# A fused block with paged attention on one core: two chunks of transposed heads per store, and the output weights on another DMA queue

## The chip, the cores and the metric

The kernel runs on one core of a Trainium2 chip. The metric is device time in microseconds of one execution, as the median of several runs. Beside it one execution was recorded by the hardware profiler; its span runs from its first to its last instruction. The engines are called by the profile's names: PE (matmul), PEld (its weight loads), DVE, ACT, POOL, and SP, which only issues DMAs here. A row "SPq" or "ACTq" is a DMA issue on that engine's instruction stream.

## The reference

There are 32 sequences of 32 tokens with 512 features. Four layers are each added to their input:

```python
x = x + einsum('bct,bcd->bdt', x, W0[cond])                    # token mixing, one of 16 matrices
x = x + x @ W.T + 0.5 * (x @ A[label]) @ Bw.T                  # base weights and a low-rank part
x = x + einsum('bsi,boi->bso', x, W2[adapter])                 # one of 8 adapters per sequence
# attention: 32 query heads, 8 key heads of 128, 512 cached keys in 16 pages of 32, 32 new ones
q, k, v = x @ Wq.T, x @ Wk.T, x @ Wv.T
q, k = rope(rmsnorm(q) * wq, pos), rope(rmsnorm(k) * wk, pos)
scores = q @ concat(k_cache[block_table], k).T / sqrt(128)     # cached keys beyond the length masked
x = x + (softmax(scores) @ concat(v_cache[block_table], v)) @ Wo.T
```

All of it is in float32.

## The kernel before, in words

The 1024 token rows are held as `NT` = 8 tiles of 128 rows, so that one tile holds `BT` = 4 sequences. The program has two stages, called A and attention below.

**Stage A** first computes the first three layers and then the projections. The projected width is cut into 12 chunks of 512 columns (`NCH`): chunks 0 to 7 are queries, 8 and 9 are keys, 10 and 11 are values. One chunk holds four heads (`REP`). Query and key chunks are computed in pairs of chunks by pairs of tiles. One such block takes seven products (`M_ORDER`) instead of eight, the results of which are added up on ACT, DVE and POOL. `BLOCKS` lists 20 blocks: the first pair of chunks is that of the keys (8, 9), the other four are queries. Time is counted in slots, one per product, seven per block. `at(slot, ...)` files a piece of work under a slot, and `flush(slot)` issues what is filed there. The queues of PE, DVE, ACT, POOL and SP follow that order as written.

A block yields four units: two chunks (`c0`, `c1`) for two tiles. `formed`, `by_cos`, `by_sin` and `rotated` make the rotated heads `u.a` of a unit (128 tokens by four heads of 128). `store_heads` (line 484) then transposes them on DVE in squares of 32 (line 489) into a tile `st`, of which there are four, and stores them with four DMAs, one per sequence, from SP (line 498). They go to a scratch array in DRAM, `q_d` for queries and `k_d` for keys, which is laid out with the head dimension first, as attention needs it. For a block that begins at slot g, the four query units are stored at g+6, g+9, g+11 and g+13; key units at g+9, g+11, g+14 and g+15. Every fourth chunk, `store_inverses` also writes the norms of the queries to `r_d` (line 459). Among the same slots SP loads the key pages of sequences 0 and 1 (`load_page`, line 199). ACT issues the stores of projected values (`v_d`, line 326) and the loads of weight pairs (`w_pair`).

**Attention** is one loop over `n`, a step per sequence `b` and key head `g`: 256 steps, and eight more (`LAG`) in which the last ones drain. A step issues, in this order: the transfers of a coming sequence; the scores of (b, g) on PE (lines 998, 999); the masked copy of them on DVE (line 1007) and the exponential on ACT (line 1023); `fill`, a matmul pair of the projection of the last value chunk, left over for steps up to 36 (line 318), whose result ACT copies and stores; the loads of output weights; `place`, which transposes a quarter of the probabilities of four steps ago on DVE (line 1036) and copies it on ACT, POOL and DVE into `placed` (lines 1048, 1050, 1052); `share`, a piece of the output projection (line 1153), from step 37 (`BEGIN`); and the products of the probabilities with the values of eight steps ago (line 1076).

What SP issues in the steps of sequence b: at its first step the second half of its queries `qt` (line 229), four pieces of new values `vn` (line 268), the new keys of b+1 (line 224) and 12 of the 16 key pages of b+1 (line 199), for which it reads page numbers from a table; at its fifth step the first half of the queries of b+1, four pieces of the norms `rq` (line 236), the remaining four pages and the next table. POOL issues the gathers of cached values `vt` (line 256). Keys and values have two sets of buffers, one for even and one for odd sequences.

**The output weights** are held in two tiles: `wos[0]` with the rows of the first 20 of 32 positions, `wos[1]` with the last 12. Each is loaded in 16 parts (`load_wo`, line 895), one per (r, k), where r picks a group of 32 partitions and k one of four rows in turn. A part of the first tile is 320 KB, of the second 192 KB. The memory of `wos[0]` was part of stage A's (among it the tiles `st`), so its first load has to wait until that is free. `WO_AT` (line 1208) says in which steps parts of the first tile are loaded: two in each of steps 4 to 8, one in steps 10, 14, 18, 22, 26 and 30, all of them issued from ACT. The second tile is loaded from SP, one part per step, from step 37 on.

Of the kernel before, what the change touches and what calls it, by code (L numbers as in the profile page):

```python
# [20 lines left out]
P = 128  # L21
# [17 lines left out]
QUAD = 4  # L39
# [20 lines left out]
def cond_resid_kernel(  # L60
# [420 lines left out]
                u.a[:, h, :], u.a[:, h, :], AF.Copy, scale=u.ss[:, h : h + 1]  # L481
            )

    def store_heads(u):
        c, t, a = u.c, u.t, u.a


        st = tp.tile([P, D // S, REP, S], F32, tag="st", name=f"st_{c}_{t}", bufs=4)
        nc.vector.transpose(
            st.rearrange("p k h s -> p h k s"), a.rearrange("p h (k d) -> p h k d", d=S)  # L490
        )
        if c < HQ // REP:
            dst, c0 = q_d, c * REP * S
        else:
            dst, c0 = k_d, (c - HQ // REP) * REP * S
        for j in range(BT):
            r = slice(j * S, (j + 1) * S)
            nc.sync.dma_start(
                out=dst[t * BT + j, :, c0 : c0 + REP * S].rearrange("(k d) x -> d k x", d=S),
                in_=st[r].rearrange("p k h s -> p k (h s)"),  # L500
            )

# [9 lines left out]
    def block(n: int, i: int, p: int):  # L512
        c0, c1 = PAIRS[i]
        u11, u12 = unit(n, c0, 2 * p), unit(n, c1, 2 * p)
        u21, u22 = unit(n, c0, 2 * p + 1), unit(n, c1, 2 * p + 1)
        q = u11.q
        b = SimpleNamespace()
        g = 7 * n

        def begin(m):  # L520
            if m in (2, 4):
                pool = ps_n
            else:
                pool = ps_m
            return pool.tile([P, HID], F32, tag="mm", name=f"m{m}_{i}_{p}")

        def out_of(name, ps, tag, bufs):
            t = rp.tile([P, HID], F32, tag=tag, name=f"{name}_{i}_{p}", bufs=bufs)
            nc.scalar.copy(t, ps)  # L529
            setattr(b, name, t)  # L530

        def mm(m):
            if m == 1:
                b.X = begin(1)
                product(b.X, i, p, 1)
            elif m == 5:
                b.Z = begin(5)
                product(b.Z, i, p, 5)
            elif m in (2, 4):
                ps = begin(m)  # L540
                setattr(b, "Y" if m == 2 else "W", ps)
                product(ps, i, p, m)
            else:
                product(b.Z if m == 3 else b.X, i, p, m, True)

        V, G = nc.vector, nc.gpsimd

        at(g + 1, lambda: out_of("r1", b.X, "r", 2))
        at(g + 2, lambda: out_of("r5", b.Z, "r5", 1))
        at(g + 3, lambda: formed(u11, b.r1, b.Y, V))  # L550
        at(g + 3, by_cos, u11)
        at(g + 4, lambda: out_of("r2", b.X, "r", 2))
        at(g + 4, by_sin, u11, 0)
        at(g + 4, by_sin, u11, 1)
        at(g + 5, lambda: formed(u12, b.r2, b.Z, V))
        at(g + 5, by_cos, u12)
        at(g + 5, rotated, u11)
        at(g + 6, lambda: out_of("r3", b.X, "r", 2))
        at(g + 6, by_sin, u12, 0)
        at(g + 6, by_sin, u12, 1)  # L560
        at(g + 7, lambda: formed(u21, b.r3, b.W, V))
        at(g + 7, by_cos, u21)
        at(g + 7, lambda: formed(u22, b.r3, b.r5, G))
        at(g + 8, rotated, u12)
        at(g + 8, by_sin, u21, 0)
        at(g + 8, by_cos, u22)
        at(g + 9, by_sin, u21, 1)
        at(g + 9, by_sin, u22, 0)
        at(g + 10, by_sin, u22, 1)
        at(g + 10, rotated, u21)  # L570
        at(g + 11, rotated, u22)
        if q:
            for u, o, hs in (
                (u11, 5, (0, 1, 2)),
                (u11, 6, (3,)),
                (u12, 7, (0, 1, 2)),
                (u12, 8, (3,)),
                (u21, 8, (0,)),
                (u21, 9, (1, 2)),
                (u21, 10, (3,)),  # L580
                (u22, 10, (0, 1)),
                (u22, 11, (2, 3)),
            ):
                at(g + o, squares, u, hs)
            at(g + 6, store_heads, u11)
            at(g + 9, store_heads, u12)
            at(g + 11, store_heads, u21)
            at(g + 13, store_heads, u22)
            half, odd = divmod(c1, QUAD)
            if odd == QUAD - 1:  # L590
                for t in (2 * p, 2 * p + 1):
                    at(g + 12, query_roots, half, t)
                    at(g + 13, query_inverses, half, t)
                    at(g + 13, store_inverses, half, t)
        else:
            for u, o in ((u11, 5), (u12, 7), (u22, 10), (u21, 11)):
                at(g + o, squares, u)
                at(g + o + 1, key_sums, u)
                at(g + o + 2, key_roots, u)
                at(g + o + 2, key_inverses, u)  # L600
                at(g + o + 3, key_scales, u, G if u is u22 else nc.scalar)
                at(g + o + 4, store_heads, u)
        if n + 1 < len(BLOCKS):
            at(g + 6, load_factors, n + 1, 0 if BLOCKS[n + 1][0] else 1, BLOCKS[n + 1][1])
        return mm
# [283 lines left out]
    def wo(h: int):  # L889
        return wos[0][:, h, :] if h < HQ - LATE else wos[1][:, h - (HQ - LATE), :]  # L890

    def load_wo(i: int, r: int, k: int, eng=nc.sync):
        g0 = i * (HQ - LATE) // REP
        w = wos[i][r * S : (r + 1) * S].rearrange("d (g k) o -> d g k o", k=REP)[:, :, k, :]
        eng.dma_start(out=w, in_=w_o4[r, k][:, g0 : g0 + w.shape[1], :])

    vnp = ctx.enter_context(tc.tile_pool(name="b_vn", bufs=2, side="right"))
    qp = ctx.enter_context(tc.tile_pool(name="b_q", bufs=2, side="right"))
# [306 lines left out]
    EMPTY = tuple(n for n in range(LAG + 2, FILLED) if n % 2 == 0)  # L1205
    EMPTY = EMPTY[: FILLED - len(fills)]
    filled = {}
    WO_AT = dict.fromkeys(range(QUAD, LAG + 1), 2) | dict.fromkeys(range(10, 31, 4), 1)
    wo_parts = [divmod(i, REP) for i in range(REP * REP)]

    def fill(n: int):
# [15 lines left out]
    with tc.manual_schedule(engines=order):  # L1227
        for n in range(N + LAG):
            b, g = divmod(n, HK)
            if n == FILLED:  # L1230
                pa.close()
                late = ctx.enter_context(tc.tile_pool(name="b_w", bufs=1))
                places.append(late)
                wos[1] = late.tile([P, LATE, HID], F32, name="wo_1")
            if BEGIN <= n <= N and n % (BT * HK) == 0:

                load_residual((n - BEGIN) // (BT * HK))
            if n < N:
                if g == 0 and b >= 1:
                    load_queries(b, 1)  # L1240
                    load_new_values(b)
                if g == 0 and 1 <= b < B - 1:
                    load_keys(b + 1)
                    keys = Picked(nc.sync, k_cache, pages_of.pop(b + 1), page_keys(b + 1), K_SHAPE)
                    load_new_keys(b + 1)
                    keys.transfer(slice(0, 12))
                if g < L // P and b >= 2:
                    load_value_chunk(b, g)
                if g == QUAD and b < B - 1:
                    load_queries(b + 1, 0)  # L1250
                    load_inverses(b + 1)
                    if b >= 1:
                        keys.transfer(slice(12, NPP))
                    if 1 <= b < B - 2:
                        load_table(b + 2)
                scored = scores(b, g)
                exponentials(*scored)
            flip_kept(n)
            fill(n)
            if n == QUAD + 1:  # L1260
                load_new_values(0)
            if n in WO_AT:
                for _ in range(WO_AT[n]):
                    load_wo(0, *wo_parts.pop(0), nc.scalar)
            if 0 <= n - FILLED < REP * REP:
                load_wo(1, *divmod(n - FILLED, REP))
            if QUAD <= n < N + QUAD:
                bq, i = divmod(n - QUAD, HK)
                q, j = divmod(i, QUAD)
                if j == 0:  # L1270
                    gather_new(bq, q)
                if j == 2:
                    flip_new(bq, q)
                place(bq, q, j)
            share(n)
            if n >= LAG:
                values(*units[n - LAG])
            if n < N and g == HK - 1 and b < B - 1:
                see_keys(b + 1)
            if n > N + QUAD:  # L1280
                at = 4 * (n - N - QUAD - 1)
                finish(NT - 1, range(at, at + 4))
        assert not dens and not prs and not pos and not placed and not pns
        load_residual(NT - 1)
        flip_kept(N + LAG)
        finish(NT - 1, range(3 * QUAD, HALF))
        finish_by_halves(NT - 1)
# [76 lines left out]
```

## Time and profile before

| | |
|---|---|
| Median of 3 runs | 1187.63 us (1181.24 to 1188.65) |
| Profiled execution, its time | 1189.01 us |
| Its span | 1187.2 us |
| PE, DVE, ACT, POOL busy | 96%, 68%, 63%, 47% of the span |
| Mean granted PE clock | 0.978 |
| Attention's first scores | 374.87 us |
| Bytes read and written in DRAM | 220.07 MB, 29.49 MB |

An engine's busy share is an average over stages with different limits, and PE's counts matmuls whose ends are modelled. The chain that ended last is PE for 50% of the span, and the rest of it is hardly split. So the page's line of 40 slices and busy times by stretch say more than the shares.

In the answers quoted below, a line of a timeline is: start in us, duration in us, engine, line, operation, tiles (written <- read), count of instructions merged, and in brackets the idle time before it and what ended it. A line of waits is: who waited, for whom, us in total, times, longest. The releaser is inferred: where the engine or transfer named has nothing to do with the instruction, something stands before it in the same queue.

### The profile page before, as it was taken

How to read it: one execution, taken by the hardware profiler on the slowest of the kernel's cores; microseconds unless marked ns; L12 is line 12 of the kernel's file. 1: busy time of each engine (PE TensorE's matmuls, PEld its weight loads, DVE VectorE, ACT ScalarE, POOL GpSimd, SP SyncE). 2: the span in 40 equal slices, each digit the busy share in tenths (PEclk: the TensorE clock that was granted, in tenths of full speed). 3: DMA queues.
4: the chain of work that ended last, by engine and by line, in shares of the span. 5: the costliest groups of instructions: out<-in, count | busy, mean ns of one | idle time of the engine just before them, and what ended most of it. 6: DMA issues, size and time to landing. Idle time of an engine off the chain costs nothing.

```text
span 1187.2 us, 19830 instructions
## 1 busy us (share of the span) xinstructions
PE 1137.2 (96%) x5432; PEld 737.7 (62%) x5432; DVE 807.1 (68%) x1670; ACT 751.6 (63%) x1900; POOL 554.3 (47%) x709
## 2 busy tenths in 40 slices
PE   8999999999999388899899999999999999999998
PEld 5543444444444176677677777777777777777766
DVE  2510788898775256677577778778877877877860
ACT  1211477666666176677577877777777777877760
POOL 3400788998985343334343443344344344333410
PEclk9999999999999698899899999999999999999999
DMA  8997456755465667689767667766776776776710
GB/s 325 389 407 305 171 138 209 220 118 161 103 178 141 165 165 228 202 264 247 213 210 238 218 220 230 242 218 211 260 218 197 257 224 197 241 238 206 225 46 10
DMA packets 193426, 250.93 MB, mean 211 GB/s; under 512 B 33794, under 2 KB 153218, under 8 KB 187554
## 3 DMA queue, kind: packets, MB, share of 16 engines
q1 hardware_dynamic: 166818, 160.64, 44.0%
q0 software_dynamic: 19216, 69.35, 17.5%
q10 hardware_dynamic: 7280, 19.66, 5.1%
q8 instruction: 44, 0.72, 0.2%
q14 instruction: 68, 0.56, 0.2%
HBM read 220.07 MB, written 29.49 MB: 210 GB/s over the span
## 4 chain that ended last, share of the span: by engine, by line
PE 50%; SPq 3%; DVE 2%; issue 1%; DMA 1%; POOL 0%; ACT 0%; ACTq 0%; DVEq 0%
PE f_ps L1153 16%; PE o_ps L1076 15%; PE s_ps L998 9%; PE s_ps L999 7%; PE o_ps L1096 1%; SPq L199 1%; DMA kt<-in_k_cache_dram 1%; SPq L187 1%; DVE turned L1036 1%; SPq L236 1%; PE f_ps L1173 1%; PE f_ps_last L1173 1%; DVE ot L1133 0%; PE pn_ps L1063 0%; DVE pr L1007 0%
## 5 line engine op out<-in xcount | busy, mean ns | idle before, releaser
L1048 ACT COPY placed<-turned 32x512 f32<-32x512 f32 x539 | 332.1, 616 | 55.8 <-DVE turned L1036 23.0
L1076 PEld LDWEIGHTS o_ps<-vt,placed 128*128 128x128 f32 x2048 | 270.8, 194 | 125.7 <-issue 98.1
L1007 DVE CUSTOM_DVE_ANT_0 pr<-s_ps,mask,rq 128x544 f32<-128x544 f32 x256 | 200.6, 784 | 153.9 <-PE s_ps L999 145.7
L1076 PE MATMUL o_ps<-vt,placed 128*128 128x128 f32 x2048 | 274.4, 278 | 10.2 <-ACT placed L1048 3.2
L1050 POOL COPY placed<-turned 32x512 f32<-32x512 f32 x268 | 163.5, 610 | 256.2 <-DVE turned L1036 197.4
L1023 ACT ACTIVATE pr<-pr,low 128x544 f32<-128x544 f32 x256 | 191.6, 748 | 140.7 <-DVE low L1007 137.0
L1153 PE MATMUL f_ps<-wo,ot 128*128 128x512 f32 x480 | 242.2, 596 | 0.7
L1036 DVE STREAM_TRANSPOSE turned<-pr 128x512 f32<-128x512 f32 x256 | 178.5, 697 | 20.6 <-ACT placed L1048 14.2
L998 PE MATMUL s_ps<-kt,qt 128*128 128x288 f32 x512 | 177.4, 429 | 10.2 <-DVE low L1007 7.8
L999 PE MATMUL s_ps<-kt,qt 128*128 128x256 f32 x512 | 155.6, 386 | 4.4 <-issue 3.1
L256 POOL DMA_INDIRECT vt<-in_v_cache_dram,v_idx x128 | 127.3, 995 | 34.6 <-issue 23.7
L999 PEld LDWEIGHTS s_ps<-kt,qt 128*128 128x128 f32 x512 | 98.6, 194 | 34.3 <-issue 7.1
L432 POOL TENSOR_TENSOR ra<-ra,rs 128x512 f32<-128x512 f32 x80 | 102.8, 1291 | 11.7 <-DVE rs L427 10.1
L1153 PEld LDWEIGHTS f_ps<-wo,ot 128*128 128x128 f32 x480 | 86.1, 191 | 28.7 <-issue 13.6
L1059 POOL COPY pq<-pr 128x128 f32<-128x128 f32 x64 | 18.5, 289 | 179.0 <-PE o_ps L1076 94.8
L1052 DVE COPY placed<-turned 32x512 f32<-32x512 f32 x217 | 95.2, 438 | 5.5
L998 PEld LDWEIGHTS s_ps<-kt,qt 128*128 128x128 f32 x512 | 78.9, 194 | 25.6 <-DVE low L1007 17.7
L445 ACT ACTIVATE sq<-x 128x128 f32<-128x128 f32 x256 | 76.2, 300 | 17.4 <-DVE x L403 14.8
L529 ACT COPY r<-m 128x512 f32<-128x512 f32 x80 | 46.3, 580 | 54.5 <-PE m L387 53.6
L387 PE MATMUL m<-t_pair,x_sums 128*128 128x512 f32 x160 | 75.3, 593 | 0.1
L387 PE MATMUL m<-w_pair,x3t 128*128 128x512 f32 x160 | 75.2, 592 | 0.0
L318 PE MATMUL qkv<-wq,x3t 128*128 128x512 f32 x128 | 62.8, 614 | 11.3 <-ACT vs L325 11.3
(128 smaller groups left out, 1232.5 us busy)
## 6 DMA issues: line engine op xcount, KB each, us to landing
kt<-in_k_cache_dram SPq DMA_DIRECT2D x512, 128.0 KB
wa<-in_w_adapt_dram SPq DMA_DIRECT2D x32, 1024.0 KB
q_d<-st SPq DMA_DIRECT2D x256, 64.0 KB
qt<-q_d SPq DMA_DIRECT2D x64, 256.0 KB
w_pair<-in_w_qkv_dram ACTq DMA_DIRECT2D x8, 1024.0 KB
wo<-in_w_o_dram ACTq DMA_DIRECT2D x16, 320.0 KB
v_d<-vs ACTq DMA_DIRECT2D x16, 256.0 KB
k_d<-st SPq DMA_DIRECT2D x64, 64.0 KB
```

Source lines behind the costliest of these rows:

```text
L256: nc.gpsimd.indirect_dma_start(out=vts[b][:, c, :], out_offset=None, in_=v_cache, in_offset=bass.IndirectOffsetOnAxis(ap=v_idx[:, at : at ...
L387: nc.tensor.matmul(ps, of[:, k], by[:, k], start=(not more and k == 0), stop=(k == KH - 1), skip_group_check=more,)
L432: nc.gpsimd.tensor_tensor(u.a, u.a, u.s, ALU.add)
L998: nc.tensor.matmul(ps[:, first:L], q, kt4[:, :N_LOW, g, :], start=True, stop=True)
L999: nc.tensor.matmul(ps[:, L : first + LT], q, kt4[:, N_LOW:, g, :], start=True, stop=True)
L1007: nc.vector.tensor_tensor_reduce(pr, ps[:, first : first + LT], mask, rqs[b][:, g // QUAD, u : u + 1], 3.0e38, ALU.add, ALU.min, low,)
L1023: nc.scalar.activation(pr, pr, AF.Exp, bias=low, scale=-1.0, accum_out=dens[quad][:, u : u + 1])
L1036: nc.vector.transpose(part, pr)
L1048: nc.scalar.copy(dst, src)
L1050: nc.gpsimd.tensor_copy(dst, src)
L1076: nc.tensor.matmul(po, pt[:, c, :], vt[:, c, g * D : (g + 1) * D], start=(c == 0 and q == 0), stop=(c == L // P - 1 and q == 1),)
L1153: nc.tensor.matmul(pfs[t][:, :HID], ots[t, h // HALF][:, h % HALF, :], wo(h), start=(h == 0), stop=(h == (HQ if t < NT - 1 else HALF) - 1),)
```

## The change

Two things are changed. `store_heads` becomes `turn_heads`: the first of the two chunks of a block transposes its heads into one half of a tile that is twice as wide, and the second chunk transposes into the other half and then stores both. The four DMAs carry 128 KB each instead of 64 KB, in runs of 1 KB instead of 512 bytes. There are two tiles `st` of twice the size instead of four. The slots stay.

The loads of the first tile of output weights are issued by SP instead of ACT, at the same place within a step, and in other steps: two in each of steps 3 to 7, then one in steps 12, 16, 20, 24, 28 and 32.

```diff
-    def store_heads(u):
-        c, t, a = u.c, u.t, u.a
-        st = tp.tile([P, D // S, REP, S], F32, tag="st", name=f"st_{c}_{t}", bufs=4)
+    turned_heads = {}
+
+    def turn_heads(u):
+        key = u.n, u.t
+        st = turned_heads.pop(key, None)
+        last = st is not None
+        if not last:
+            st = turned_heads[key] = tp.tile(
+                [P, D // S, 2 * REP, S], F32, tag="st", name=f"st_{u.n}_{u.t}", bufs=2
+            )
+        c0 = u.c - u.c % 2
+        h = (u.c - c0) * REP
         nc.vector.transpose(
-            st.rearrange("p k h s -> p h k s"), a.rearrange("p h (k d) -> p h k d", d=S)
-        )
-        if c < HQ // REP:
-            dst, c0 = q_d, c * REP * S
+            st[:, :, h : h + REP, :].rearrange("p k h s -> p h k s"),
+            u.a.rearrange("p h (k d) -> p h k d", d=S),
+        )
+        if not last:
+            return
+        if u.q:
+            dst, x0 = q_d, c0 * REP * S
         else:
-            dst, c0 = k_d, (c - HQ // REP) * REP * S
+            dst, x0 = k_d, 0
         for j in range(BT):
             r = slice(j * S, (j + 1) * S)
             nc.sync.dma_start(
-                out=dst[t * BT + j, :, c0 : c0 + REP * S].rearrange("(k d) x -> d k x", d=S),
+                out=dst[u.t * BT + j, :, x0 : x0 + 2 * REP * S].rearrange(
+                    "(k d) x -> d k x", d=S
+                ),
                 in_=st[r].rearrange("p k h s -> p k (h s)"),
             )
...
-    def load_wo(i: int, r: int, k: int, eng=nc.sync):
+    def load_wo(i: int, r: int, k: int):
...
-        eng.dma_start(out=w, in_=w_o4[r, k][:, g0 : g0 + w.shape[1], :])
+        nc.sync.dma_start(out=w, in_=w_o4[r, k][:, g0 : g0 + w.shape[1], :])
...
-    WO_AT = dict.fromkeys(range(QUAD, LAG + 1), 2) | dict.fromkeys(range(10, 31, 4), 1)
+    WO_AT = dict.fromkeys(range(3, LAG), 2) | dict.fromkeys(range(12, 33, 4), 1)
...
-                    load_wo(0, *wo_parts.pop(0), nc.scalar)
+                    load_wo(0, *wo_parts.pop(0))
```

More of the change, by code (lines that the diff above doesn't have):

```diff
@@ L584, in block @@
                 at(g + o, squares, u, hs)
[L585 to L588, printed above, removed]
+            at(g + 6, turn_heads, u11)
+            at(g + 9, turn_heads, u12)
+            at(g + 11, turn_heads, u21)
+            at(g + 13, turn_heads, u22)
             half, odd = divmod(c1, QUAD)
@@ L601, in block @@
                 at(g + o + 3, key_scales, u, G if u is u22 else nc.scalar)
-                at(g + o + 4, store_heads, u)
+                at(g + o + 4, turn_heads, u)
         if n + 1 < len(BLOCKS):
```

## The prediction

> **What bounds the kernel now.** I read the page's 40 slices first, then busy time by stretch, then who waited for whom inside the weak stretch, then the timelines of ACT, SP and PE there. The slices say where to look (PE busy and granted PE clock, in tenths, 29.7 us a slice):
>
> ```profile
> PE   8999999999999388899899999999999999999998
> PEclk9999999999999698899899999999999999999999
> ```
>
> PE is full until slice 13 (386 to 415 us), where it is 3 tenths busy. That is the start of attention, and the slices up to 19 are thin too. From slice 20 on PE is full again. By stretch (us, then PE, PEld, DVE, ACT, POOL busy, clock, DMA share, GB/s):
>
> ```profile
> 320.00:360.00 40.00, 40.00 (x95) 17.76 (x94) 29.12 (x55) 26.58 (x134) 34.64 (x35) 1.00 0.65 170
> ...
> 392.00:420.00 28.00, 6.99 (x16) 4.22 (x17) 3.99 (x8) 7.59 (x16) 5.35 (x9) 0.54 0.81 194
> 480.00:500.00 20.00, 18.29 (x86) 13.54 (x83) 11.74 (x24) 14.50 (x29) 8.32 (x13) 0.76 0.53 146
> ```
>
> In 392 to 420 every engine is mostly idle, so something is being waited for that is no engine's work. ACT's waits from 386 to 500 us (total, times, longest):
>
> ```profile
> ACT placed L1048 <- DMA vn<-v_d: 16.8, 2, 11.0
> ...
> ACT pn L1065 <- DMA kt<-in_k_cache_dram: 14.2, 3, 4.9
> ACT placed L1048 <- DMA kt<-in_k_cache_dram: 4.0, 1, 4.0
> ```
>
> A copy from `turned` to `placed` has no use for `vn`. ACT's timeline shows what stands before it:
>
> ```profile
> 385.30 0.75 ACT L1023 ACTIVATE pr<-pr,low 128x544 f32<-128x544 f32 x1 [0.87 <-DVE low L1007]
> ...
> 392.67 4.43 ACTq L895 DMA_DIRECT2D wo<-in_w_o_dram  x2
> 397.14 0.62 ACT L1048 COPY placed<-turned 32x512 f32<-32x512 f32 x1 [11.00 <-DMA vn<-v_d]
> ...
> 409.23 1.06 ACTq L895 DMA_DIRECT2D wo<-in_w_o_dram  x2
> 410.33 0.27 ACT L1065 COPY pn<-pn_ps 128x128 f32<-128x128 f32 x1 [4.54 <-DMA kt<-in_k_cache_dram]
> ```
>
> The compiled program of the kernel before says why. Each DMA from SP or ACT waits for the DMA eight before it, counted over both queues together. The first `wo` load also waits for the last stores of stage A, whose memory it takes. The trace's landings fit to the hundredth: inverses (`r_d`) landed at 392.52 and the first load issued at 392.67; a `vn` piece at 403.92, the fourth load at 403.94; a page of keys at 409.21, the fifth at 409.23. So ACT stands still on DMAs that SP issued late, with copies and exponentials behind it, and PE behind those: 7.8, 11.1 and 2.6 us of PE idle up to 417, and 2.5 and 2.7 us at 449 and 477.
>
> The pace without that, from PE's steps (a step runs from one L998 group to the next):
>
> ```profile
> 433.18 0.65 PE L998 MATMUL s_ps<-kt,qt 128*128 128x288 f32 x2
> ...
> 435.15 0.75 PE L998 MATMUL s_ps<-kt,qt 128*128 128x288 f32 x2
> 435.74 0.59 PE L999 MATMUL s_ps<-kt,qt 128*128 128x256 f32 x2
> 436.18 1.02 PE L318 MATMUL qkv<-wq,x3t 128*128 128x512 f32 x2
> 437.03 1.05 PE L1076 MATMUL o_ps<-vt,placed 128*128 128x128 f32 x8
> 437.92 0.65 PE L998 MATMUL s_ps<-kt,qt 128*128 128x288 f32 x2
> ```
>
> That is 1.97 us without and 2.77 with a value projection; 2.07 in steps 0 to 7. Step 0 starts at 374.87, step 8 at 399.3, 16 at 437.9, 24 at 465.7, 32 at 494.9, 40 at 517.9. At PE's own pace step 40 would come at 391.5 (step 8) + 20.4 + 19.7 + 19.7 + 21.2 = 472.5. So 45 us are lost before step 40. After it a block of 8 steps takes 22.8 us and PE is full, so whatever shift step 40 has is the shift of the end.
>
> **Part 1, stores joined.** 320 stores of 64 KB become 160 of 128 KB. SP's rows give 0.438 us an issue: per stage A block 16 x 0.438 = 7.0 us become 3.5 of the 12.04 us that a block takes (7 products whose matmul groups begin 1.72 us apart in the timeline). SP is late now; its tail shows it:
>
> ```profile
> 368.03 11.23 SPq L498 DMA_DIRECT2D q_d<-st  x12
> 379.36 0.87 SPq L459 DMA_DIRECT2D r_d<-rq  x2
> 380.32 10.17 SPq L498 DMA_DIRECT2D q_d<-st  x16
> 390.60 0.86 SPq L459 DMA_DIRECT2D r_d<-rq  x2
> 391.56 0.38 SPq L229 DMA_DIRECT2D qt<-q_d  x1
> ```
>
> The last transpose ends at 385.89. Its four stores and two inverses now end issue by 388.6 instead of 391.5 and land by about 390.1. A 64 KB store lands 1.8 us after issue, a 128 KB key page 2.1; I take 2.1. The 80 transposes keep number and shape. Their output steps differ, but L489, L1036 and L1133 write three layouts in 0.704, 0.697 and 0.705 us, so nothing is added. Stage A itself gains nothing: PE is 40.00 of 40 there.
>
> The two tiles of 4 KB leave less room than four of 2 KB. A tile was free again four transposes later, one block (12 us). Now its stores must land 4 or 5 slots of 1.72 us after the second transpose (6.9 to 8.6 us), and 2 or 3 slots where key blocks meet query blocks. Undisturbed, second transpose to landing would be 4 x 0.44 + 2.1 = 3.9 us. I cost this at nothing: DVE is 29.1 of 40 busy, and PE's accumulators let DVE be some 5 us late. Without that cover it is the third case below.
>
> **Part 2, output weights on SP.** ACT loses 16 issues of 0.32 us and, above all, the 16.8 + 14.2 + 4.0 = 35.0 us of standing. What is late next is SP. Its order from step 3: two loads, `qt` (0.43), four `rq` (2.5), two loads, four `vn` (2.5), six loads; then at step 8 `qt`, `vn`, the page numbers, new keys and 12 pages; at step 12 `qt`, `rq`, four pages, one load. The 10 loads cost 0.43 to 0.45 us each (the later `wo` set on SP: 0.428), 4.5 in all. From 390.1: 390.1 + 4.5 + 0.4 + 2.5 + 2.5 = 400.0 for the `qt` of step 8. From that `qt` to the last key page landed took 23.8 us in block 4 (493.3 to 517.1), so block 2's keys would land at 423.8. Ten 320 KB loads also have to land: those issued last, together, landed 1.5 us apart, so the tenth lands near 409, and the second page, eight behind it, waits for it. That adds 1 to 4 us. I take 426 for step 16, against 437.9.
>
> From there SP sets the pace, not PE (19.7 us a block): 23.8 less 2.3 of landing, plus 0.35 for the page table and 0.9 for two loads is 22.8 us a block. Three blocks: 426 + 68.4 = 494.4; step 40 came 0.8 after its keys, so 495.2 against 517.9. That is 22.7; I take off 2, since such a block would carry 5.9 MB (17 key pieces of 131 KB, four value chunks of 524, two `qt` and two `wo`, `vn`, one `v_d`) at 259 GB/s, as fast as the stretch 520 to 560 went (262 GB/s at 0.90 share). **Gain 21.** Between the ends: keys spaced by the shortest seen (20.1, blocks 7 to 8) and step 16 at 424 give 28; keys spaced as where eight late loads ran beside them (25.6 and 27.2) and step 16 at 430 give 10.
>
> The profiled run took 1189.01 us with a span of 1187.2, 1.4 above the median of 1187.63. Less 21: 1168.0 for such a run, 1166.6 for the median; I say 1167.
>
> [...] Here 2.66 us idle before 479.50 is followed by the 0.76 of the stretch 480 to 500. [...]
>
> **The rivals.** *The keys set those blocks already* (0.15). Keys of blocks 2 to 5 landed 26.4, 28.3 and 29.2 us apart. If SP and the transfers made that spacing, only step 16's shift and little else is kept: about 8, 1180. For it: latencies of 5 to 6.5 us for block 5's pages at 500. Against it: SP's own longest waits there,
>
> ```profile
> SPq L229 <- PE s_ps L999: 26.6, 6, 8.9
> ```
>
> SP stood for PE's scores, so PE was the later one.
>
> *Stage A starves on two tiles* (0.13), the slower side. DVE stands at a transpose until stores land, up to 12 us after it where SP is late (185 to 213, 228 to 243, 272 to 290, 332 to 380). If SP stays as late as now, the second transposes of those pairs exceed 7.7 us by some 40 us in sum, less about 2 us a block that DVE has spare, so PE loses near 30, plus half-clock time; net of the 21, 12 to 15 slower, near 1201. It decides once the waits take over 21 us from PE. Against it: half the stores, so SP keeps up.
>
> *SP doesn't bind* (0.06): pages overlap with loads, gain over 30, near 1155.
>
> **How the numbers follow.** Forecast 0.66, 1160 to 1178. With the first rival the range reaches 1184 and down to 1157, leaving out the slower case and little more. About 1% (11.9 us) is what can be told from no change: faster 0.74, within 0.13, slower 0.13.
>
> **What would show it.** Right: no ACT wait at a `placed` or `pn` copy on a DMA; steps 0 to 7 unchanged; a PE wait at step 16 for keys or `low`; last store issued near 387.6. Wrong: DVE `st` waiting on `q_d<-st` for more than 10 us in all, PE below 39 of 40 in stage A, or keys landing more than 25 us apart in blocks 2 to 5.

## The result, and the profile after

| | before | after |
|---|---|---|
| Median | 1185.41 us (15 runs, 1179.44 to 1189.11) | 1190.97 us (15 runs, 1188.20 to 1195.06) |
| Profiled execution, its span | 1189.01, 1187.2 us | 1188.20, 1186.4 us |

The ratio of the times is **1.0047**, with an interval of 1.0031 to 1.0063. The change is half a per cent slower; by the bound of 1% that the prediction set, this is "within 1%". The forecast was 1167, so about 21 us that were expected did not come.

The two profiled executions differ the other way by 0.8 us: that of after is the fastest of its 15 runs, that of before lies near the slow end of its own. So the half per cent itself can't be read from this pair. What can be read is where the expected 21 us went. First the slices, PE busy and granted PE clock in tenths, 29.7 us each:

```profile
PE   9999999999999767799999999999999999999998
PEclk9999999999999878899999999999999999999999
```

The hole of slice 13 is filled (7 tenths where it was 3), but slices 14 to 16 are at 6, 7 and 7 where they were at 8. In the changed kernel the lines behind `turn_heads` have numbers higher by 12 (L1048 is now L1060, L895 is L907); the stores of `st` are at L508, its transposes at L496. By stretch, with the columns used before (us, then PE, PEld, DVE, ACT, POOL busy, clock, DMA share, GB/s):

```profile
320.00:360.00 40.00, 40.00 (x95) 17.73 (x94) 28.44 (x54) 26.67 (x133) 34.13 (x35) 1.00 0.71 189
392.00:420.00 28.00, 19.60 (x104) 14.91 (x103) 10.36 (x23) 13.46 (x28) 9.72 (x17) 0.82 0.72 176
480.00:500.00 20.00, 13.02 (x66) 10.62 (x67) 10.16 (x22) 10.45 (x23) 8.94 (x13) 0.83 0.59 170
```

Stage A is as full as before. From 392 to 420 PE does 19.6 us of work where it did 7.0; from 480 to 500 it does 13.0 where it did 18.3. The gain is made and then given back. The starts of the steps say where (us):

| step | 0 | 8 | 16 | 24 | 32 | 40 | 64 | 255 |
|---|---|---|---|---|---|---|---|---|
| before | 374.9 | 399.3 | 437.9 | 465.7 | 494.9 | 517.9 | 593.9 | 1138.6 |
| after | 373.9 | 391.2 | 425.5 | 458.4 | 488.5 | 518.7 | 594.2 | 1137.8 |

A step is counted here from its first group of scores (L1010, L998 before), which reads nine of the 17 pieces of keys. The second group (L1011, L999 before) reads the other eight, among them the pages that are loaded last, and it tells more. PE's timeline in the kernel after:

```profile
411.14 1.30 PE L1010 MATMUL s_ps<-kt,qt 128*128 128x288 f32 x2 [7.93 <-DMA qt<-q_d]
...
425.48 0.72 PE L1010 MATMUL s_ps<-kt,qt 128*128 128x288 f32 x2 [2.05 <-DVE mask L219]
435.74 1.22 PE L1011 MATMUL s_ps<-kt,qt 128*128 128x256 f32 x2 [9.54 <-DMA kt<-in_k_cache_dram]
```

and the second group of step 16 in the kernel before:

```profile
438.41 0.59 PE L999 MATMUL s_ps<-kt,qt 128*128 128x256 f32 x2
```

At step 10 the changed kernel leads by 25.2 us (397.66, before 422.86), more than the 21 that were forecast. At step 12 PE waits 7.9 us for queries, at step 16 it waits 9.5 us for the last keys. The first group of step 16 still leads by 12.4 us, the second by 2.7 only, and at step 40 nothing is left. ACT's waits from 386 to 500 us (who, for whom, total, times, longest):

```profile
ACT pr L1035 <- DVE low L1019: 49.4, 17, 12.8
ACT placed L1060 <- DVE turned L1048: 2.2, 6, 0.4
ACT placed L1060 <- ACT vs L325: 1.6, 4, 0.4
```

All 35 us that ACT stood for DMAs at `placed` and `pn` are gone; nearly all that is left is waiting for scores (`low` comes from them), and so for PE. SP's waits from 374 to 540 us:

```profile
SPq L236 <- DMA v_d<-vs: 16.4, 2, 8.6
SPq L907 <- DMA v_d<-vs: 7.4, 2, 4.0
SPq L229 <- DMA v_d<-vs: 5.0, 1, 5.0
SPq L199 <- DMA v_d<-vs: 4.2, 1, 4.2
```

These are 33.0 us of standing. The kernel before has 7.0 of that kind in the same stretch, at the last stores of stage A, and none at what attention loads; there its SP waited mainly for PE's scores. Not one of these four lines issues a DMA that reads `v_d`: L236 loads norms, L907 output weights, L229 queries, L199 key pages. What they wait for are the stores of the left-over value projections, which ACT issues when PE has done that `fill`. SP's timeline around the longest:

```profile
446.98 0.42 SPq L907 DMA_DIRECT2D wo<-in_w_o_dram  x1
447.49 0.38 SPq L229 DMA_DIRECT2D qt<-q_d  x1
456.53 2.48 SPq L236 DMA_DIRECT2D rq<-r_d  x4
459.21 0.97 SPq L199 DMA_DIRECT2D kt<-in_k_cache_dram  x2
```

and ACT's in the same microseconds:

```profile
453.66 0.56 ACT L325 COPY vs<-qkv 128x512 f32<-128x512 f32 x1
454.26 0.33 ACTq L326 DMA_DIRECT2D v_d<-vs  x1
```

SP issues nothing from 447.87 to 456.53. ACT issues the store of value tile 5 at 454.26, after PE's `fill` of 451.88 to 452.90 and the copy; it lands at 456.47, and 0.06 us later SP goes on. The trace shows the order: the 1196 DMAs that SP and ACT issue signal eight semaphores in turn, in one cycle over both queues (1356 on the same eight in before), and each is issued only after the last signal that the trace has of the DMA eight before it. In this common order the store stands eight before the first `rq` of sequence 3. In the kernel before it stands behind those `rq`, and the next that waits for it is the first key page of the sequence after, which was issued at 470.65, 6.8 us after the store had landed. The other stands fit in the same way: stores landed at 388.14, 395.18, 421.47, 486.58 and 512.46, SP issued at 388.21, 395.19, 421.48, 486.65 and 512.47. So PE's progress now holds up the transfers that PE needs next:

```profile
PE s_ps L1011 <- DMA kt<-in_k_cache_dram: 23.9, 3, 9.5
PE s_ps L1010 <- DMA qt<-q_d: 7.9, 1, 7.9
```

That view is PE's waits from 374 to 520 us. The wait for queries is the one at step 12, for the `qt` that SP issued at 401.14, behind two of these stands. The three waits for keys end at 435.74, 466.52 and 496.03, at the start of blocks 2, 3 and 4; the keys of blocks 2 to 5 landed 30.7, 29.4 and 25.0 us apart.

### The profile page after: what moved, and what is told of

Read it like the earlier page. It is cut to its first block, busy times and chain, and to the rows that moved or that the text cites. A ratio compares the mean times of both kernels' runs of the same rounds, so it can differ in the third digit from the quotient of the medians.

```text
span 1186.4 us, 19557 instructions
## 1 busy us (share of the span) xinstructions
PE 1133.7 (96%) x5432; PEld 738.8 (62%) x5432; DVE 804.0 (68%) x1670; ACT 751.5 (63%) x1900; POOL 553.1 (47%) x709
## 4 chain that ended last, share of the span: by engine, by line
PE 83%; DMA 5%; SPq 4%; DVE 3%; issue 2%; POOL 1%; ACT 1%; ACTq 0%; DVEq 0%; POOLq 0%
PE m L387 17%; PE o_ps L1088 17%; PE f_ps L1165 16%; PE s_ps L1010 10%; PE s_ps L1011 9%; PE qkv L318 4%; PE adapt L742 2%; PE base L717 2%; DMA kt<-in_k_cache_dram 2%; PE o_ps L1108 2%; SPq L236 1%; SPq L199 1%; DMA qt<-q_d 1%; DVE pr L1019 1%; SPq L907 1%
## 5 line engine op out<-in xcount | busy, mean ns | idle before, releaser
L1060 ACT COPY placed<-turned 32x512 f32<-32x512 f32 x539 | 332.1, 616 | 33.5 <-DVE turned L1048 24.9
L1010 PE MATMUL s_ps<-kt,qt 128*128 128x288 f32 x512 | 176.1, 426 | 11.3 <-DMA qt<-q_d 7.9
L1011 PE MATMUL s_ps<-kt,qt 128*128 128x256 f32 x512 | 157.0, 389 | 30.4 <-DMA kt<-in_k_cache_dram 28.6
L1048 DVE STREAM_TRANSPOSE turned<-pr 128x512 f32<-128x512 f32 x256 | 178.6, 698 | 0.1
L1011 PEld LDWEIGHTS s_ps<-kt,qt 128*128 128x128 f32 x512 | 98.6, 194 | 60.8 <-issue 20.3
L1010 PEld LDWEIGHTS s_ps<-kt,qt 128*128 128x128 f32 x512 | 78.5, 193 | 26.2 <-DVE low L1019 9.6
L387 PE MATMUL m<-w_pair,x_sums 128*128 128x512 f32 x160 | 72.2, 593 | 0.0
```

What stands on the lines that cost most here:

```text
L387: nc.tensor.matmul(ps, of[:, k], by[:, k], start=(not more and k == 0), stop=(k == KH - 1), skip_group_check=more,)
L1010: nc.tensor.matmul(ps[:, first:L], q, kt4[:, :N_LOW, g, :], start=True, stop=True)
L1011: nc.tensor.matmul(ps[:, L : first + LT], q, kt4[:, N_LOW:, g, :], start=True, stop=True)
L1048: nc.vector.transpose(part, pr)
L1060: nc.scalar.copy(dst, src)
```

## The experiments

The theory (A): the value stores that stand ahead of SP's loads in the common order cost what was to be gained, and each stand is lost by itself. The rival (B): the blocks are as long as their transfers take, late key pages and POOL's gathers of values running at once; the stands only fill time in which SP would have had nothing to gain. The ratios are to runs of the kernel before on the same chip.

**Which half of the change does it.** Joined stores alone (the weights stay with ACT, in the old steps), and the weights alone:

```diff
-    def load_wo(i: int, r: int, k: int):
+    def load_wo(i: int, r: int, k: int, eng=nc.sync):
...
-        nc.sync.dma_start(out=w, in_=w_o4[r, k][:, g0 : g0 + w.shape[1], :])
+        eng.dma_start(out=w, in_=w_o4[r, k][:, g0 : g0 + w.shape[1], :])
...
-    WO_AT = dict.fromkeys(range(3, LAG), 2) | dict.fromkeys(range(12, 33, 4), 1)
+    WO_AT = dict.fromkeys(range(QUAD, LAG + 1), 2) | dict.fromkeys(range(10, 31, 4), 1)
...
-                    load_wo(0, *wo_parts.pop(0))
+                    load_wo(0, *wo_parts.pop(0), nc.scalar)
```

> The stores joined as in the change, the output weights left on ACT in the steps of before. Theory A (the ring: with the weights on SP, the program's common order of DMAs puts ACT's value stores of steps 13, 21, 29 and 36 ahead of SP loads that PE needs before or soon after those steps, so SP, ACT and PE wait for one another): here those stores stand behind SP's norms again, as in before, so SP does not stand for them; ACT stands at its weight loads as in before (over 25 us from step 4 to step 36), step 8 some 0 to 8 us earlier than before, step 40 within 6 us of before's 517.9, time within 6 us of before. Theory B (the transfers: ten weight loads and the value gathers fill the DMA engines, so keys land late whatever the order): the same here, since the weights are spread as in before. Theory C (stage A starves on two store tiles): step 0 over 3 us later than 374.9 and the time over 4 us slower than before.

> The weights moved to SP as in the change, the stores as in before. Theory A: the value stores of steps 21 and 29 stand ahead of the norms of steps 20 and 28 in the common order here too, so SP stands 6 to 10 us twice and step 40 comes at 515 to 525; time 1 to 10 us slower than before. Step 8 is later than the change's 391, at 395 to 400, since SP ends its stores later. Theory B: the same slowness, but from latencies of 5 us and more of the last key pages, without SP standing for a value store.

(The second is the kernel before with the last two of these edits the other way round.) Joined stores alone: 1181.22 us, ratio 0.9944 [0.9922, 0.9967]. Step 8 comes at 391.7 instead of 399.3, and 3.6 us of that are left at step 40 (514.3). ACT still stands for DMAs, 29.7 us from 386 to 500. The gain is just over the 6 us that were expected at most. Weights alone: 1195.86 us, ratio 1.0066 [1.0042, 1.0091], with step 8 at 401.6 and step 40 at 525.6, both about a microsecond later than expected. SP's waits there from 374 to 540 us:

```profile
SPq L236 <- DMA v_d<-vs: 17.5, 2, 10.0
SPq L498 <- DMA v_d<-vs: 8.9, 3, 5.8
SPq L895 <- DMA v_d<-vs: 6.2, 2, 4.2
SPq L199 <- DMA v_d<-vs: 3.8, 1, 3.8
```

The 8.9 us at L498 are the last stores of stage A, which waited 7.0 us in the kernel before too. The other stands for value stores come with the weights, not with the joined stores: with joined stores alone SP has none in attention. What the move to SP does and what the new steps of the loads do was not tried apart.

**The value stores off the common order.** Nothing is changed but the queue of the six value stores of attention's `fill` (tiles 2 to 7); POOL issues them, and POOL's DMAs are not in that order (in the traces of before and after its 137 signal eight other semaphores):

```diff
-    def store_values(ps, c: int, t: int):
+    def store_values(ps, c: int, t: int, eng=nc.scalar):
...
-        nc.scalar.dma_start(out=v_d[t * P : (t + 1) * P, c0 : c0 + HID], in_=vs)
+        eng.dma_start(out=v_d[t * P : (t + 1) * P, c0 : c0 + HID], in_=vs)
...
-                store_values(filled.pop(t), NCH - 1, t)
+                store_values(filled.pop(t), NCH - 1, t, nc.gpsimd)
```

> The change, with the value stores of attention's projections issued from POOL instead of ACT; nothing else differs, and no store of another engine stands in SP's order in attention. Theory A: SP's stands at 416, 448 and 479 us are gone, steps 24, 32 and 40 come at or before 452, 477 and 502 (458.4, 488.5, 518.7 in the change), time 1170 to 1179. Theory B: the keys still land 27 us and more apart, step 40 at 510 to 519, time 1186 to 1192.

1163.37 us, ratio **0.9789** [0.9756, 0.9823]: faster than both kernels, and than theory A had it (1170 to 1179). Step 16 comes at 416.6 and step 40 at 491.5. SP's longest waits from 374 to 540 us are now

```profile
SPq L229 <- PE s_ps L1011: 3.6, 2, 3.4
SPq L268 <- DMA wo<-in_w_o_dram: 2.8, 3, 1.1
```

and the issue that took 8.66 us of waiting goes out at once:

```profile
434.96 0.39 SPq L229 DMA_DIRECT2D qt<-q_d  x1
435.45 2.49 SPq L236 DMA_DIRECT2D rq<-r_d  x4
```

By the ratios, one edit of queue is worth 0.9789 / 1.0047 = 0.974, some 30 us (24.5 between the two profiled spans).

**Two of the stores, and the others.** If each stand costs by itself, some of the stores can be taken off, and the loss must go from the blocks that belong to them:

```diff
-                store_values(filled.pop(t), NCH - 1, t)
+                store_values(filled.pop(t), NCH - 1, t, nc.gpsimd if t in (5, 6) else nc.scalar)
```

> The change, with two of attention's six value stores (those of steps 21 and 29) issued from POOL, the other four left on ACT at their places in the common order. Theory A: exactly the two stands of SP of 8.6 and 7.8 us before the norms of steps 20 and 28 go, the ones at 383, 417 and 508 us stay. Step 16 as in the change (425.5), step 24 at 448 to 454, step 32 at 472 to 480, step 40 at 497 to 506; time 1173 to 1181, between the change (1191) and the run with all six on POOL (1163). Theory B or a gain that comes from POOL's queue as such: little or none until all six are moved, 1186 to 1192.

> The complement of the run that moved tiles 5 and 6: value stores of tiles 2, 3, 4 and 7 from POOL, those of 5 and 6 from ACT. Theory (each stand of SP for a value store costs by itself): SP's stands at the page of step 16 and at the first queries of steps 4 and 36 go, the two at the norms of steps 20 and 28 stay at 14 to 19 us in sum; step 16 as early as with all stores on POOL (416 to 419), and the rest of what moving all gave: step 40 at 518.7 less (27.2 less 10.7) = 502, ratio 0.984 to 0.990. Rival (only the two long stands cost, the other moves are worth nothing, and the 40 to 64 stretch takes what is left): step 40 at 514 to 519, ratio 1.000 to 1.005.

The second has the opposite choice. Tiles 5 and 6 from POOL: 1184.11 us, ratio 0.9930 [0.9906, 0.9953]. All others from POOL: 1175.15 us, ratio 0.9904 [0.9875, 0.9933]. Waits of SP, in the first

```profile
SPq L907 <- DMA v_d<-vs: 9.3, 2, 5.6
SPq L229 <- DMA v_d<-vs: 5.2, 1, 5.2
SPq L199 <- DMA v_d<-vs: 4.1, 1, 4.1
```

and in the second

```profile
SPq L236 <- DMA v_d<-vs: 13.5, 2, 6.9
```

In attention, each has the stands of the stores that it left with ACT and, but for 1.3 us at a weight load in the second, no others for value stores. Time from step to step, from first group to first group (us):

| value stores from POOL | 8 to 16 | 16 to 24 | 24 to 32 | 32 to 40 | 40 to 64 |
|---|---|---|---|---|---|
| none (after) | 34.3 | 32.9 | 30.1 | 30.2 | 75.5 |
| 5 and 6 | 34.3 | 33.0 | 21.3 | 27.7 | 83.3 |
| all but 5 and 6 | 25.5 | 27.8 | 30.4 | 32.3 | 74.4 |
| all | 24.9 | 29.3 | 21.3 | 24.3 | 78.5 |

The stand at the norms of sequence 3 (tile 5) is lost in steps 24 to 32, that at the norms of sequence 4 (tile 6) in 32 to 40, those of tiles 2 to 4 in steps 8 to 24: taking a store off the order shortens the blocks that belong to it and no earlier one. The gains over after add up, too: 1.0047 less 0.9930 is 0.0117, less 0.9904 is 0.0143, together 0.0260; all at once gave 0.0258, where each ratio is known to 0.003. Both runs were slower than expected, the second just: it reached step 40 at 508.3 instead of 502, since its two stands cost 9.2 and 8.0 us in their blocks against the run without any. In the first, 10.7 us were won by step 40 and most of that was given back between steps 40 and 64 (83.3 us instead of 75.5). Why it was given back stays open; its profiled execution, at 1188.71 us, was also the slowest of its eight. The price expected for the first run was wrong, its mechanism was seen.

**Is POOL's queue a gain by itself?** The same edit of the value stores, with the weights on ACT: with joined stores (which closes the table), and on the kernel before.

> The fourth corner of the table weights on ACT or SP by value stores on ACT or POOL, all with joined stores. Theory (a value store that stands ahead of SP's loads in the common order is the cost): with the weights on ACT no value store holds SP up for long, so taking these stores out of the order removes little; ACT still stands at its weight loads for 25 to 35 us in all, step 40 at 508 to 516, ratio 0.990 to 0.999. Rival (value stores issued from POOL are a gain wherever they are, 0.974 as between the changed kernel and the one with its value stores on POOL): 0.9944 x 0.974 = 0.969, step 40 below 495.

> The kernel before, with attention's value stores issued from POOL: output weights on ACT, stores by single chunks. Theory A: in before these stores stood behind SP's norms and held nobody, so moving them gives little; ACT still stands at its weight loads (35 us from 386 to 500). Step 8 at 399, step 40 at 510 to 518, time 1178 to 1188, at most 1% faster. If moving the value stores were good in itself, whatever queue the weights are on, it would come near the 24 us that it gave on top of the change: 1160 to 1167.

| joined stores, weights on | value stores from ACT | from POOL |
|---|---|---|
| ACT | 0.9944 [0.9922, 0.9967] | 0.9925 [0.9899, 0.9952] |
| SP | 1.0047 [1.0031, 1.0063] | 0.9789 [0.9756, 0.9823] |

On the kernel before: 1189.04 us, ratio 0.9987 [0.9966, 1.0008], a microsecond slower than the range expected. Where the weights are on ACT, moving the value stores is worth little or nothing; where they are on SP, it is worth 2.6%. With joined stores and the weights on ACT, step 40 comes at 506.7 (508 to 516 was expected, below 495 by the rival), and ACT goes on standing, a little less than expected (its waits on SP's loads from 386 to 500 us):

```profile
ACT pn L1077 <- DMA kt<-in_k_cache_dram: 12.8, 3, 5.5
ACT placed L1060 <- DMA vn<-v_d: 8.1, 1, 8.1
ACT placed L1060 <- DMA kt<-in_k_cache_dram: 3.0, 2, 1.7
```

So either move alone leaves the two queues tied: with the weights on ACT, ACT stands for SP's loads; with the weights on SP and the value stores on ACT, SP stands for ACT's stores. Together they untie them.

**Spread loads.** On the version with all value stores from POOL, one weight load in each of steps 3 to 18 instead of two in each of steps 3 to 7:

```diff
-    WO_AT = dict.fromkeys(range(3, LAG), 2) | dict.fromkeys(range(12, 33, 4), 1)
+    WO_AT = dict.fromkeys(range(3, 19), 1)
```

> The change with all six value stores on POOL and the 16 weight loads one per step in steps 3 to 18 instead of ten in steps 3 to 7 and six later. The term under test: ten loads in a row hold up the second queries of sequence 1 (issued 394.5, landed 404.6 with the stores on POOL; 9.9 us in the change). Spread, they should land within 6 us, and the first key pages of sequence 2 follow earlier; but six more loads fall before step 19. Theory A: step 40 within 5 us of the 491.5 without the spread, time 1158 to 1168. If the ten loads in a row cost what they add to that latency (6 us): 1157 to 1160. If the transfers themselves are what binds: 1166 to 1172.

1177.96 us, ratio 0.9892 [0.9862, 0.9922], slower than without this edit and outside all three ranges that were expected (1157 to 1172). PE busy falls to 17.65 of 32 us in the stretch 428 to 460:

```profile
392.00:428.00 36.00, 28.66 (x158) 21.90 (x158) 19.03 (x41) 22.03 (x45) 17.41 (x28) 0.91 0.89 218
428.00:460.00 32.00, 17.65 (x90) 13.16 (x88) 12.67 (x28) 13.82 (x28) 9.82 (x15) 0.76 0.84 235
```

Four of the loads, issued from 417.6 to 418.9 beside POOL's gathers, land only from 426.9 to 434.5; the `qt` of step 16, issued at 419.4 behind them, lands at 435.1, and the last page of keys for step 24 at 459.9. So with the value stores on POOL, spreading the ten loads gains nothing; with eleven of the 16 among the key pages and gathers (steps 8 to 18) the kernel is slower. That it is this company that makes the transfers late is an argument from these rows.

**The gathers later.** For the rival B, POOL's gathers of cached values were moved two steps back, away from the late key pages:

```diff
-                if g < L // P and b >= 2:
-                    load_value_chunk(b, g)
+                if 2 <= g < 2 + L // P and b >= 2:
+                    load_value_chunk(b, g - 2)
```

> The change, with POOL's gathers of cached values two steps later in each sequence (steps 2 to 5 of 8 instead of 0 to 3), so that they no longer start with the last key pages in flight. Theory A: the last pages of sequences 2, 3 and 4 land 2 to 3 us after issue instead of 5 to 8, which gives at most 3 to 10 us by step 40, while SP's stands of 8 us near steps 20 and 28 remain; time 1181 to 1189. Theory B: keys land 25 us apart or less, step 40 at 500 to 508, time 1172 to 1180. Later gathers may also make the values late for the step that needs them, which would show as PE waiting for vt.

1234.65 us, ratio 1.0401 [1.0367, 1.0435]. This doesn't test what it was to test. From step 64 to 255 it takes 582 us instead of 544, and POOL's copies now stand behind the gathers (POOL's waits from 560 us on):

```profile
POOL placed L1062 <- DMA vt<-in_v_cache_dram,v_idx: 98.7, 23, 6.1
```

The kernel after has no such row, and PE waits 27.3 us for these copies there. Up to step 40 it can be read: step 40 at 518.3, with 518.7 in after, and PE's waits for keys 21.4 us against 23.9. Moving the gathers has not shortened those blocks, but what the late pages lose to them stays open.

**The kernel before once more**, for a second profile:

> The kernel before once more, for a second profile: how far two profiles of one kernel differ. Step 8 within 2 us of 399.3, step 40 within 4 us of 517.9, the span within 6 us of 1187.2.

Steps 8, 16 and 40 come at 399.1, 437.1 and 518.4 (399.3, 437.9 and 517.9 in the first), so the readings by step above hold to about a microsecond.

## Why the prediction was wrong

**The bound** was right: ACT stood at the weight loads for DMAs that SP issued late, and with the loads gone from ACT all of it went. PE leads by 25.2 us at step 10.

**Stage A** was right as to PE: 40.00 of 40 busy, step 0 at 373.9. DVE waits for stores of `st` 3.0 us in all (the bound set was 10), and a transpose still takes 0.704 us, so the rival "Stage A starves on two tiles" is refuted (that PE's accumulators let DVE be some 5 us late was the author's estimate; no run shows it). The term behind it was mis-sized. The prediction let the last transpose end at 385.89 as before and put the last store at 387.6. SP's tail in the kernel after:

```profile
374.30 5.51 SPq L508 DMA_DIRECT2D q_d<-st  x8
379.92 0.88 SPq L459 DMA_DIRECT2D r_d<-rq  x2
382.29 0.82 SPq L907 DMA_DIRECT2D wo<-in_w_o_dram  x2
388.21 0.34 SPq L229 DMA_DIRECT2D qt<-q_d  x1
```

The last transposes stand 9 us earlier in DVE's order (the last begins at 376.5, before at 385.2), and SP could issue the first weight load at 382.29, not at 390.1. Joined stores alone show the same: step 8 at 391.7.

**Step 16** began at 425.5 where 426 was said, and that is luck. The 426 stood for the landing of block 2's keys, and those landed at 435.70; what began at 425.5 was the group that does not need the last pages. Of the prediction's signs of being right, the wait for keys at step 16 did come, 9.5 us long, in a kernel that gained nothing. The way there was off in each part. SP was free at 382.29, 7.8 us earlier than said. From there to the `qt` of step 8 the prediction counted 9.9 us of issue; the trace has 382.29 to 401.14, 18.9 us: those 9.9, two stands for value stores, 5.0 at `qt` and 3.4 at a weight load, and 0.6 of other waits. From that `qt` to the last key page landed it had 23.8 us and 1 to 4 more; the trace has 34.6, with a third stand of 4.2 at a page and a last page that took 8.5 us to land. With all value stores from POOL, the keys landed at 423.57, 12.1 us earlier.

**The step that failed** is "From there SP sets the pace", and the sum for step 16 ahead of it, which goes by the same rule. It priced a block at what SP has to issue, 22.8 us, and so took for granted that SP waits for nobody. The part on the bound had just explained that ACT stood because its DMAs wait for SP's; the sum then moved 16 loads to the other queue and did not ask where that puts ACT's remaining DMAs in the common order. "What is late next is SP" named the right queue with the wrong reason: SP was late for ACT's stores, which are tied to PE's own steps, and stood 33.0 us for them. So the keys were not in time for the steps after. From second group to second group, blocks 2 to 4 took 30.8, 29.5 and 24.9 us, as far apart as their keys landed. With the stands taken away they take 22.7, 22.8 and 22.8 us, 68.3 in all, where the prediction had 68.4, and step 40 comes at 491.5 where it had 495.2. That fit is closer than the mechanism: at step 24 of that run the keys had landed 4.4 us before PE came to them (441.98 and 446.42), so SP did not set that block. The forecast pace thus belongs to the kernel with the value stores from POOL, not to this one. Why the changed kernel is half a per cent slower than before, and not equal, stays open.

**The first rival** came nearest: keys 25 us and more apart. But it gave transfers as the cause and 1180 as the price, and kept step 16's shift. Of the 85.2 us of blocks 2 to 4, 16.9 went with the value stores taken off the order; what is left is the 68.3 above. **"SP doesn't bind"** fell. No case in the prediction had an order between the queues turned round, and so none gave more than the time before except by a starved stage A.

**"Whatever shift step 40 has is the shift of the end"** holds for after and for the run with all value stores from POOL (26.4 us earlier at step 40, 25.2 at step 255). It fails where tiles 5 and 6 alone were moved and for the kernel before with its value stores from POOL (6.2 us earlier at step 40, 0.8 later at 255). In the fastest version the stretch 520 to 560 has

```profile
520.00:560.00 40.00, 33.58 (x189) 25.04 (x188) 25.73 (x57) 24.76 (x51) 10.71 (x17) 0.91 0.90 262
```

There PE is not full, at a DMA share of 0.90, with the second set of weights loading from step 37 on. Whether the transfers are the limit there was not shown: the kernel before has PE busy for 39.07 of 40 us in the same stretch, at the same share of 0.90 and 262 GB/s.

**The issuing queue and the clock.** The measured 1.0047, taken alone, looks as if the move of the loads were worth about nothing. The runs say otherwise: with the same DMAs and the same bytes, the choice of the issuing engine moved the time between 0.9789 and 1.0047, since waits of SP and ACT on each other come with it (33.0 us of SP's standing in attention in after). How the granted clock follows PE's waits no run settled. The waits in after that ended at 435.74 and 466.52 (9.5 and 7.5 us) stand beside a clock of 0.80 from 428 to 460 and of 0.83 from 460 to 490. The kernel before has a second short wait like the 2.66 us ahead of 479.50 that the prediction named: 2.50 us, ended at 451.90, and the next pair of L998 took 1.33 us where 0.65 to 0.75 is usual, at a granted clock of 0.53 from 451.90 to 453.50.

## What to carry to other kernels

Where the DMAs of two engines share one order of waits, as SP's and ACT's do here at a depth of eight, a load that is moved from one engine to the other moves every other DMA of both against each other: before pricing the move, look at what then stands one depth ahead of each load on the critical path, and whether its issuer can only issue it once the bottleneck engine has come further. SP's pace of issue, 22.8 us a block, was not the block here: blocks 2 to 4 took 30.8, 29.5 and 24.9 us. A store that depends on the bottleneck's own progress is better kept out of an order in which the next loads stand behind it: here that was worth 2.6%, and little or nothing where no such load stood behind it. If an expected gain appears at first and is gone some steps later, compare the starts of the steps and then ask the late queue itself what it waited for.

## What was not expected of the hardware

Some loads landed late though nothing held up their issue any more: the `qt` of step 8, issued at 401.14 behind ten 320 KB loads, landed after 9.9 us, and that of step 16 in the run with spread loads after 15.7 us. The last key pages of blocks 2, 3 and 4 in after, which start while POOL's gathers run, landed 8.5, 5.5 and 4.8 us after issue, where a page in a quiet stretch (issued at 414.58) took 2.1 us.
